# Turning v to rows in an attention block: one product of 64x128 of the array for four batches, in place of four of 64x32

## The chip, the cores and the metric

The kernel runs on one core of one Trainium2 chip. Its time is the device time of one execution in microseconds. The core has five engines with instruction streams of their own: TensorE (PE, matrix products; its weight loads are listed as PEld), VectorE (DVE), ScalarE (ACT), GpSimd (POOL) and SyncE (SP, which here only issues DMAs). They wait for each other by semaphores.

## The reference

One transformer block with adaptive layer norm, for 4 batches of 1024 steps of 256 channels:

- h = layernorm(x), scaled and shifted per batch
- q, k, v = silu(causal convolution with 4 taps of a projection of h to 1024 channels), that is 16 heads of 64; k is normalised; alpha and beta are sigmoids of projections of h
- a recurrence over the steps for each batch and head, on a 64x64 state S:

```
v_old = S k
S     = clip(alpha * S + beta * (v - alpha * v_old) k^T, -5, 5)
o     = S q
```

- o times a silu gate, a projection back to 256 channels, and a gated residual sum
- a second layer norm, a mixture of 8 experts of which each row uses 2, and a gated residual sum

## The kernel before

The kernel does the recurrence in 32 chunks of 32 steps. Two chunks, an even one (par 0) and an odd one (par 1), form a pair. Within a chunk the steps are solved at once through a triangular system, so that a chunk is a series of small matrix products and the state is carried from chunk to chunk. After the recurrence (function chunks, up to about 1890 us) follows the experts' part (function blocks), and after it two fallbacks that run only if the clip was in danger of acting.

The function chunks writes the order of the work itself: the scheduler is off for TensorE, VectorE, ScalarE and GpSimd (manual_schedule), and the letters of the string PLAN (line 56) say which of several generators takes its next step. In each of the 16 rounds, streams of two ages run side by side: passes (c), bounds (b) and below (l) finish the present pair, while rows, decays, keys_and_queries, values, triangle, rows_of_k and scaled (n, d, k, v, t, h, s) prepare the next one. SP's DMA issues are placed by the framework's scheduler.

The tiles that matter here hold four batches b of 32 steps, in one of two layouts. "Channels" has the channels of two heads on the partitions, a head p in each half of 64, and (batch, step) along the row: kq and v. "Rows" has (batch, step) on the 128 partitions, so that batch b is the quadrant of partitions 32b to 32b + 31 (quads), and the channels along the row: z, u, o. A product with a 64-row operand uses half of the rows of the array, and one with 32 columns of weights uses a quarter of its columns; the profile writes this as 64*32.

Steps that the change and the prediction touch, by line:

- L431, L441, L443, L449: projections and convolutions of k, q and v (ps_q on TensorE, then ScalarE and VectorE, then silu on ScalarE). L579 and L586: the gate's product, and its silu on ScalarE.
- L888 (in passes): v is turned to rows into ps_z, two PSUM tiles of 128x512, one per half p. The weights are v itself, the moving operand is a 64x64 identity. This opens an accumulation that L903 finishes with the product of k and the state; L912 copies it to z.
- L753, L756, L758 (end of triangle, VectorE): the solved triangular system and r_r are transposed.
- L810 and L822 (below): products of 32x32 and smaller for the off-diagonal blocks of the triangular solution; L810 needs Tn and the end of the VectorE steps above.
- L923, L937, L955, L974: u, the state's part of the output, the update of the state, the rest of the output. L1009: the output is transposed. L1025: the projection back.
- L352, L377, L378: the router's small products. L1063: u is transposed for the bounds. L1056: two loads per bounds step from a scratch tensor (aR, kR).

In an even chunk L888 is issued after L1009 of the chunk before and is followed by L810. In an odd chunk it is issued between a projection (L431) and a gate product (L579).

Of the kernel before, what the change touches and what calls it, by code (L numbers as in the profile page):

```python
# [212 lines left out]
def chunks(ctx, tc, a, nch, con, ones, modt, modc, x1_dram, n_safe, rt):  # L213

    nc = tc.nc
    GA, SB, CB = 0, 1, 2
    ident, iota8 = con["ident"], con["iota8"]
# [38 lines left out]
    half_p = lambda p: slice(p * 64, p * 64 + 64)  # L256
    quads = [slice(b * 32, b * 32 + 32) for b in range(B)]
# [614 lines left out]
    class Chunk:  # L872
# [3 lines left out]
        def passes(self, prev):  # L876

            pair, par, g = self.pair, self.par, self.pair.g
            kq, v, Tt, dq, kend = pair.kq, pair.v, pair.Tt, pair.dq, pair.kend[par]
# [4 lines left out]
            ps_z = [ps_c.tile([P, HP, DH], F32, name="ps_z", tag="c") for _ in range(2)]  # L884
            for hp in range(HP):
                for p in range(2):
                    for b, q in enumerate(quads):
                        nc.tensor.matmul(  # L888
                            ps_z[p][q, hp],
                            lhsT=v[hp // 2][half_p(p), hp % 2, par, b],  # L890
                            rhs=ident[half_p(p), half_p(p)],
                            start=(hp == 0),
                            stop=False,
                            skip_group_check=True,
                        )
            if par == 1:
                close("v", "v", "v", "v")
            yield
# [1 line left out]
            for hp in range(HP):  # L900
                for p in range(2):
                    for b, q in enumerate(quads):
                        nc.tensor.matmul(  # L903
                            ps_z[p][q, hp],
                            lhsT=kq[half_p(p), 0, hp, par, b],
                            rhs=S[half_p(p), b, hp],
                            start=False,
                            stop=True,
                            skip_group_check=True,
# [24 lines left out]
            for hp in range(HP):  # L934
                for p in range(2):
                    for b, q in enumerate(quads):
                        nc.tensor.matmul(  # L937
                            ps_o[p][q, hp],
                            lhsT=kq[half_p(p), 1, hp, par, b],
                            rhs=S[half_p(p), b, hp],  # L940
                            start=(hp == 0),
                            stop=False,
                            skip_group_check=True,
# [27 lines left out]
            for p in range(2):  # L971
                for hp in range(HP):
                    for q in quads:
                        nc.tensor.matmul(  # L974
                            ps_o[p][q, hp],
                            lhsT=dq[q, n_of(p, hp)],
                            rhs=u[q, hp, p],
                            start=False,
                            stop=True,
                            skip_group_check=True,  # L980
# [166 lines left out]
    def both_of(pair, prev):  # L1147
        chunks = [Chunk(pair, par) for par in range(2)]
        one = [prev] + chunks[:1]

        def passes():
            for c, before in zip(chunks, one):
                yield from c.passes(before)

        def bounds():
            for before in one:
                yield from before.bounds() if before else idle(14)

        return chunks[-1], passes(), bounds()
# [15 lines left out]
    for g in range(npair):  # L1175

        clear(3)
        prev, passes, bounds = both_of(now, prev)
        streams = dict(l=now.below(), c=passes, b=bounds, x=loads(2 * g + 6))
        if g + 1 < npair:  # L1180
            after, finished[:] = list(finished), []
            x = newer
            newer = [x_of.pop(2 * g + 4 + par) for par in range(2)] if g + 2 < npair else None
            now = Pair(g + 1, x, newer, after)
            streams.update(preparing(now))
        work(streams, PLAN)
# [721 lines left out]
```

## Time and profile before

| what | value |
|---|---|
| median of 3 runs | 2393.99 us (2391.24 to 2396.91) |
| profiled execution | 2413.01 us |
| its span, first to last instruction | 2411.1 us |
| mean granted TensorE clock | 0.826 |
| busy: PE, PEld | 1835.6 us (76%), 1491.0 us (62%) |
| busy: DVE, ACT, POOL | 1601.7 us (66%), 1008.6 us (42%), 1079.9 us (45%) |
| L888 on TensorE | 4096 records, 62.9 us busy, 21.6 us idle before them |

How to read it: the span is one execution seen by the hardware profiler; busy times of the engines overlap. A group line gives the source line, engine, operation, tiles, the part of the array (rows*columns), the shape of the moving operand, the count, then busy time in us and mean ns of one record, then the idle time of the engine before the group and what ended most of it. A record's ns includes its way through the array, and records overlap, so the rate is read from stretches, not from the mean. A line of waits gives in total us, times and longest us. A line of the timeline gives start and length in us, and in brackets the idle time before it and who ended it.

### The profile page before, as it was taken

Reading aid. Unit: us, or ns where it says so; the run is one execution under the profiler, and the core shown is the slowest. Engines: PE = TensorE matmul, PEld = TensorE weight load, DVE = VectorE, ACT = ScalarE, POOL = GpSimd, SP = SyncE. Lnnn points to the kernel's source line nnn. Section 1 sums busy time; section 2 is a strip of 40 time slices with the busy share of each in tenths; the row PEclk is TensorE's granted clock in tenths of the full one; section 3 lists DMA queues with packets and bytes.
Section 4 is the critical chain, followed back from the end, with each engine's and each line's share of the span. In section 5 each row is a group of like instructions: output and inputs, shape, how many; then the busy total and the mean of one; then the engine's idle time right before and its main releaser. Section 6 shows DMA issues by size and latency. Waiting matters only on the chain.

```text
span 2411.1 us, 96754 instructions
## 1 busy us (share of the span) xinstructions
PE 1835.6 (76%) x42550; PEld 1491.0 (62%) x42550; DVE 1601.7 (66%) x3170; ACT 1008.6 (42%) x2005; POOL 1079.9 (45%) x1189
## 2 busy tenths in 40 slices
PE   5677878787878787878687878878786716999930
PEld 3566656665767676766566666666675615888830
DVE  4768777878887868788777878897877323111124
ACT  3344545454544545455444444545443212222211
POOL 1115363637463636465545555564636450000046
PEclk7788878888978888889787979889887757999975
DMA  5513332425353434344434424242323105666636
GB/s 153 159 48 96 121 93 72 144 81 148 92 140 87 139 88 134 87 136 118 118 94 127 107 79 109 77 105 73 96 66 89 42 22 197 224 228 221 225 118 183
DMA packets 321248, 285.37 MB, mean 118 GB/s; under 512 B 112243, under 2 KB 279283, under 8 KB 320435
## 3 DMA queue, kind: packets, MB, share of 16 engines
q1 hardware_dynamic: 304946, 245.08, 35.5%
q0 software_dynamic: 9264, 27.01, 3.2%
q8 instruction: 337, 5.52, 0.9%
q10 hardware_dynamic: 6608, 7.00, 0.9%
q14 instruction: 93, 0.75, 0.1%
HBM read 215.09 MB, written 67.90 MB: 117 GB/s over the span
## 4 chain that ended last, share of the span: by engine, by line
PE 55%; issue 13%; DVE 8%; POOL 8%; DMA 7%; ACT 7%; SPq 2%; POOLq 0%; ACTq 0%; DVEq 0%
PE ps_q L431 16%; PE ps_hm L1670 6%; PE ps_yb L1682 5%; PE ps_w L1025 4%; PE ps_kk L647 3%; DMA sc<-g_scratch 3%; PE ps_gt L579 3%; PE ps_t L810 2%; PE ps_u L923 2%; PE ps_s L955 2%; POOL kq L792 2%; POOL aS L993 2%; DVE kq L443 2%; DMA y<-outs_scratch,at_out 1%; PE ps_o L974 1%
## 5 line engine op out<-in xcount | busy, mean ns | idle before, releaser
L443 DVE SCALAR_TENSOR_TENSOR kq<-ps_q,w_conv,kq 128x256 f32<-128x256 f32 x768 | 362.1, 482 | 132.8 <-ACT kq L441 112.1
L431 PE MATMUL ps_q<-hT,w_kq 128*128 128x280 f32 x1024 | 366.0, 507 | 32.4 <-issue 10.2
L431 PEld LDWEIGHTS ps_q<-hT,w_kq 128*128 128x128 f32 x1024 | 232.7, 241 | 110.2 <-issue 22.6
L443 DVE SCALAR_TENSOR_TENSOR v<-ps_q,w_conv,v 128x256 f32<-128x256 f32 x384 | 185.1, 482 | 70.4 <-ACT v L441 59.9
L441 ACT ACTIVATE kq<-ps_q,w_conv 128x256 f32<-128x256 f32 x256 | 143.5, 563 | 207.1 <-PE ps_q L431 205.0
L792 POOL TENSOR_TENSOR kq<-kq,sc 128x512 f32<-128x512 f32 x128 | 179.6, 1423 | 85.8 <-DMA sc<-g_scratch 82.3
L1096 DVE TENSOR_TENSOR_SCAN sides<-aR,sides 128x512 f32<-128x512 f32 x128 | 187.8, 1469 | 35.6 <-POOL sides L1089 34.9
L431 PE MATMUL ps_q<-hT,w_v 128*128 128x280 f32 x512 | 170.7, 461 | 36.9 <-ACT least L1073 21.7
L1088 POOL TENSOR_TENSOR sides<-sides,least 128x512 f32<-128x512 f32 x128 | 192.0, 1500 | 10.0
L1686 DVE TENSOR_TENSOR yb<-ps_yb,b 128x256 f32<-128x256 f32 x78 | 33.1, 424 | 244.2 <-PE ps_yb L1682 244.2
L993 POOL TENSOR_TENSOR aS<-S,last 128x1024 f32<-128x1024 f32 x64 | 127.1, 1986 | 137.5 <-DVE S L962 137.5
L1085 POOL TENSOR_TENSOR sides<-sides,kR 128x512 f32<-128x512 f32 x128 | 162.3, 1268 | 16.5 <-ACT sides L1071 16.4
L1677 ACT ACTIVATE hm<-ps_hm,b 128x256 f32<-128x256 f32 x156 | 73.8, 474 | 220.6 <-PE ps_hm L1670 220.5
L579 PE MATMUL ps_gt<-hT,w_gt 128*128 128x256 f32 x512 | 154.3, 427 | 4.0 <-issue 3.6
L1687 POOL DMA_DIRECT2D outs_scratch<-yb x39 | 27.9, 716 | 286.2 <-DVE yb L1686 276.5
L1670 PE MATMUL ps_hm<-hT,w 128*128 128x256 f32 x624 | 144.6, 385 | 9.1 <-DVE hT L1665 7.5
L1682 PE MATMUL ps_yb<-w,hm 128*128 128x256 f32 x624 | 141.0, 379 | 0.0
L431 PEld LDWEIGHTS ps_q<-hT,w_v 128*128 128x128 f32 x512 | 99.6, 213 | 66.3 <-ACT least L1073 31.8
L394 POOL DMA_INDIRECT rows_scratch<-ln_h,at x64 | 64.9, 1014 | 159.6 <-DVE at L391 79.9
L1670 PEld LDWEIGHTS ps_hm<-hT,w 128*128 128x128 f32 x624 | 117.9, 192 | 29.6 <-DVE hT L1665 14.2
L441 ACT ACTIVATE v<-ps_q,w_conv 128x256 f32<-128x256 f32 x128 | 72.0, 563 | 153.3 <-PE ps_q L431 150.4
L810 PE MATMUL ps_t<-Tn,kd 32*32 32x16 f32 x4096 | 63.4, 209 | 94.0 <-issue 53.8
(211 smaller groups left out, 3990.4 us busy)
## 6 DMA issues: line engine op xcount, KB each, us to landing
w<-in_w SPq DMA_DIRECT2D x78, 512.0 KB
rows_scratch<-zero_row SPq DMA_DIRECT2D x34, 1024.0 KB
w_kq<-in_w_qkv SPq DMA_DIRECT2D x260, 128.0 KB
sc<-g_scratch SPq DMA_DIRECT2D x128, 256.0 KB
w_v<-in_w_qkv SPq DMA_DIRECT2D x129, 128.0 KB
w_gt<-in_w_g SPq DMA_DIRECT2D x258, 64.0 KB
aR<-g_scratch SPq DMA_DIRECT2D x128, 128.0 KB
kR<-g_scratch SPq DMA_DIRECT2D x128, 128.0 KB
```

The source lines that it names most:

```text
L431: nc.tensor.matmul(ps.rearrange("p y t -> p (y t)"), lhsT=w[:, dc], rhs=h_t[:, dc].rearrange("p x b t -> p (x b t)"), start=(dc == 0), sto ...
L441: nc.scalar.activation(o, tap(0), AF.Identity, scale=taps[:, 0:1], bias=taps[:, KC : KC + 1])
L443: nc.vector.scalar_tensor_tensor(o, tap(j), taps[:, j : j + 1], o, op0=ALU.mult, op1=ALU.add)
L579: nc.tensor.matmul(ps, lhsT=wg[:, dc], rhs=self.h_t[:, dc, :, :, KC - 1 :].rearrange("p x b t -> p (x b) t"), start=(dc == 0), stop=(dc == 1),
L792: nc.gpsimd.tensor_tensor(o, o, sc[:, h4 : h4 + 4], ALU.mult)
L810: nc.tensor.matmul(ps[q, n], lhsT=kd[q, n], rhs=Tn[q, n], start=True, stop=True)
L993: nc.gpsimd.tensor_tensor(aS.rearrange("q b h i -> q (b h) i"), S[:, bs].rearrange("q b h i -> q (b h) i"), self.pair.last[self.par][:, bs ...
L1085: nc.gpsimd.tensor_tensor(grow, grow, kR.rearrange("q h b t -> q h (b t)"), ALU.mult)
L1088: nc.gpsimd.tensor_tensor(grow, grow, least, (ALU.subtract, ALU.add)[y])
L1096: nc.vector.tensor_tensor_scan(f, aR.rearrange("q h b t -> q (h b t)"), f, 0.0, ALU.mult, ALU.add)
L1670: nc.tensor.matmul(ps, lhsT=w1[:, dc, fc * P : (fc + 1) * P], rhs=hT[:, dc], start=(dc == 0), stop=(dc == 1),)
L1682: nc.tensor.matmul(ps, lhsT=hm[:, fc, s * P : (s + 1) * P], rhs=w2[:, fc], start=(fc == 0), stop=(fc == 3),)
```

## The change

The inner loop over the four batches goes. The four 64x32 weight operands, v[..., par, b] for b = 0 to 3, lie next to each other in a row, so they are taken as one operand of 64x128, and the output as all 128 partitions of ps_z[p] in place of one quadrant. The moving operand, the start and stop flags and the place in PLAN are as before.

```diff
             for hp in range(HP):
                 for p in range(2):
-                    for b, q in enumerate(quads):
-                        nc.tensor.matmul(
-                            ps_z[p][q, hp],
-                            lhsT=v[hp // 2][half_p(p), hp % 2, par, b],
-                            rhs=ident[half_p(p), half_p(p)],
-                            start=(hp == 0),
-                            stop=False,
-                            skip_group_check=True,
-                        )
+                    nc.tensor.matmul(
+                        ps_z[p][:, hp],
+                        lhsT=v[hp // 2][half_p(p), hp % 2, par].rearrange("q b t -> q (b t)"),
+                        rhs=ident[half_p(p), half_p(p)],
+                        start=(hp == 0),
+                        stop=False,
+                        skip_group_check=True,
+                    )
```

## The prediction

> **What bounds the kernel now.** I read first the page's span, its slices and its DMA queues.
>
> ```profile
> span 2411.1 us, 96754 instructions
> ...
> PE   5677878787878787878687878878786716999930
> ...
> q8 instruction: 337, 5.52, 0.9%
> ...
> PE 55%; issue 13%; DVE 8%; POOL 8%; DMA 7%; ACT 7%; SPq 2%; POOLq 0%; ACTq 0%; DVEq 0%
> ```
>
> The change sits in the first 1890 us, where the state is scanned in 16 rounds of about 110 us (two chunks each). TensorE is 70 to 80% busy there and holds most of the chain. The other thing to see is q8: 337 packets of 5.52 MB, so 16.4 KB each. TensorE's records are 2 x 42550 plus its waits, and 5.52 MB over these is 64 bytes each: q8 is TensorE's own instructions, arriving 256 at a time.
>
> Then the groups of the matmul engine, shapes kept apart.
>
> ```profile
> L888 PE MATMUL ps_z<-consts,v 64*32 64x64 f32 x4096 | 62.9, 269 | 21.6 <-issue 20.1 <-ACT v L449 1.1
> ```
>
> The 2048 products of L888 are 4096 records (each fp32 product runs in two passes), 128 records per chunk; with weight loads 256 instructions. "issue" is idle time that no wait explains.
>
> Then the waits, for what stands around L888:
>
> ```profile
> PE ps_t L810 <- issue: 53.8, 27, 3.1
> ...
> PE ps_t L810 <- DVE r_r L758: 35.6, 13, 5.7
> ```
>
> Last the timeline of TensorE, an even chunk (first four lines), an odd one (sixth), and rows for the costs:
>
> ```profile
> 1039.39 1.04 PE L888 MATMUL ps_z<-consts,v 64*32 64x64 f32 x62
> 1042.59 1.27 PE L888 MATMUL ps_z<-consts,v 64*32 64x64 f32 x66 [2.15 <-issue]
> 1045.73 1.04 PE L810 MATMUL ps_t<-Tn,kd 32*32 32x16 f32 x61 [1.87 <-DVE r_r L758]
> 1048.98 1.90 PE L810 MATMUL ps_t<-Tn,kd 32*32 32x16 f32 x128 [2.21 <-issue]
> ...
> 1086.91 0.61 PE L352 MATMUL ps_l<-w_router,hT 128*128 128x8 f32 x4
> 1087.45 1.16 PE L955 MATMUL ps_s<-u,kend 32*64 32x64 f32 x64
> ...
> 1091.14 0.60 PE L1063 MATMUL ps_ut<-consts,u 128*128 128x128 f32 x4
> ...
> 1102.44 1.13 PE L579 MATMUL ps_gt<-hT,w_gt 128*128 128x256 f32 x4
> ...
> 1107.98 1.75 PE L888 MATMUL ps_z<-consts,v 64*32 64x64 f32 x128
> ```
>
> In even chunks L888 is followed by L810, which waits for VectorE's transpose r_r (L758). In odd chunks it stands between a projection and the gate product L579, with nothing to wait for. The gaps of 2.15 and 2.21 us lie 66 + 61 = 127 pairs, or about 256 instructions, apart: the spacing of the q8 packets. TensorE runs out of instructions where they are short.
>
> **The change, part by part.** It replaces 64 products of 64x32 per chunk by 16 of 64x128 with the same 64 moving columns, so 128 records become 32 and 256 instructions 64. The order of TensorE, VectorE, ScalarE and GpSimd is otherwise unchanged. In SP's queue two aR loads (L1056) of one chunk pass one w_v and two w_gt issues; at 0.6 us per issue that is under 2 us, once, in a stream (bounds) that is used a chunk later: nothing, or 2 us if that cover fails.
>
> *Cost of a new record.* No 64x128 product is in the trace. Loading 128 columns of weights: L352 moves 8 columns and takes (0.61 - 0.29 for one record) / 3 = 0.11 us per record; L1063 moves 128 and takes (0.60 - 0.30) / 3 = 0.10. So at 8 moving columns it is the 128-column load that costs 0.11 us. At the half clock L1009 takes (1.97 - 0.42) / 7 = 0.22 us per record around 802 us, where the granted clock is 0.50. The new record loads 128 columns and moves 64, so it is bound by its load. The old one loaded 32, four tiles side by side; that is what the change gives away. Do the two 64-row halves load side by side? L955 has tiles in two row groups and two column halves: (1.16 - 0.23) / 63 = 15 ns per record, or 59 ns for four, hardly more than one 64-column load (half of 0.11). All four therefore load at once, row groups too. Ends: 55 ns per record with the halves side by side, 110 ns one after the other (110 and 220 at the half clock). I take 55, because L955 is the nearest row, and keep 110.
>
> [...] But L579, all in the same rows, takes (1.13 - 0.43) / 3 = 0.23 us for 256 columns, twice the 0.10 of L1063's 128, with no load added: the load is hidden. [...]
>
> *Odd chunks.* Before, sixteen stretches of L888 add up to 30.0 us in the timeline (1.57 to 2.66, mean 1.88, 0.14 of it gaps). After: 16 pairs x 0.11 + 0.3 for the last record = 2.06 us at full clock, 3.8 us for the last chunk, which runs at half: 15 x 2.06 + 3.8 = 34.7, or +4.7 us. The gate product and with it ScalarE (gate, v) come later by this; L377 behind it mostly waits 0.5 to 0.85 us for VectorE anyway. With TensorE's 55% of the chain for the share that shows: **+3 us**; ends 0 and +5.
>
> *Even chunks.* After: 16 x 0.22 + 0.4 = 3.9 us at the half clock. From the start of L888 to the end of r_r there are 4.3 to 8.7 us in the sixteen rounds (median 5.4), and L810 starts 0.1 us after r_r in nearly all. So nothing is lost, and 18 of the 20 us of gaps inside L888 that vanish were hidden by the same wait: **0**. If that cover went, it would cost 3.9 - 2.2 = 1.7 us per round.
>
> *Instruction blocks.* 4096 - 1024 = 3072 records and as many loads go: 6144 instructions, 24 of 337 packets. [...] Only what falls behind r_r counts, which is L810: 512 instructions, so two block ends in each round, most with a gap of 1.5 to 2.7 us. With 192 fewer instructions just before it, the block that L810 meets first has had longer to arrive. In the rounds at 1512 and 1617 us only one gap is left, and from L810's start to the end of L511 takes 6.6 and 6.8 us; the others take about 9.1. If each round lost one gap this would be 16 x 2.4 = 38 us; if gaps only move, 0. I take a quarter, four rounds: **-10 us**, near to the share of rounds (2 of 16) that show it, plus the odd chunks' 2 us.
>
> Sum: 3 + 0 - 10 = -7 us on the profiled span of 2411.1, so 2404 there (that execution was 2413.0). The median of the runs shown is 19 us lower, and I carry the difference over: 2394 - 7 = **2387 us**.
>
> **The rivals.** *The halves load in turn* (slower). 110/220 ns per record: an odd chunk takes 32 x 0.11 + 0.3 = 3.8 us, 1.9 more than before, x 16 x 0.55 = +17; an even one 7.1 to 7.4 us at the half clock against r_r after 4.3 to 8.7, in sum about +25 over the rounds. With the blocks' -10 that is +32: 2426 us. It is one mechanism, at L888, and decides from about 70 ns per record on (0.55 x 16 x (32 x 0.07 + 0.3 - 1.88) = 6 us in odd chunks, 2 to 4 in even ones, against 10). For it: no row shows 64x128. Against: L955.
> [...]
> *The gaps only move*: +3, 2397, no measurable change. For it: L810 keeps its 512 instructions and both of its block ends.
> *The gaps go in ten of sixteen rounds*: +3 - 24, 2373. For it: all rounds have one just behind L888.
> *The change does nothing*: excluded, for the instructions themselves differ.
>
> **How the numbers follow.** Forecast (2381 to 2393) 0.43; gaps only move 0.22; in turn 0.15; not hidden 0.12; many gaps go 0.08. About 0.2%, 5 us, is what can be told from no change. Faster: 0.36 of the forecast, the last 0.08 and 0.02 of others, 0.46. Same: 0.07 of the forecast, 0.14 of the moved gaps, 0.04 of the unhidden loads, 0.25. Slower: the rest, 0.29. The range of 2370 to 2412 leaves out the halves in turn (0.15) and the tail of the many gaps; the forecast's own range is 2379 to 2395.
>
> **What would show it.** L888 with 1024 records, an odd chunk taking 2.0 to 2.2 us, q8 with 313 packets; no more wait of L810 on L888 than before, the r_r wait longer; the issue gaps of L810 below 53.8 us. [...] The forecast is wrong if L810's gaps stay above 50 us, or if the clock falls: L888 in odd chunks runs at the full clock now.

## The result, and the profile after

The changed kernel takes 2370.79 us and the kernel before 2393.99 us (medians of 11 runs each): 23 us less, where 7 were forecast. The ratio used below is 0.9887 with a 95% interval of 0.9858 to 0.9916, 27 us; here and in every later ratio only fast runs count, which leaves out two of the 11 of the changed kernel, at 2383.9 and 2387.8 us, over 1.5% above its fastest. The profiled executions lie further apart than the medians (spans 2411.1 and 2353.9 us), since runs of one kernel differ by 0.7 to 1.7% among themselves; so single profiles are used below for what happens at one line, and timed runs for time.

The page of the changed kernel, in the lines that answer to those of before:

```profile
span 2353.9 us, 90609 instructions
...
q8 instruction: 313, 5.13, 0.9%
...
PE 52%; DVE 12%; issue 11%; ACT 8%; POOL 7%; DMA 7%; SPq 2%; ACTq 0%; POOLq 0%; DVEq 0%
```

24 instruction packets are gone, as counted, and "issue" on the chain falls from 13% to 11%.

That "issue" is mostly the wait for these packets can be read from their times in the traces. Up to 1890 us the kernel before has 133 issue gaps of TensorE over 0.4 us; 92% of them end 1.2 to 1.8 us after the end of a q8 packet (of the 107 in the changed kernel, 91%). Where two gaps lie one block of 256 instructions apart, exactly one packet stands between their ends, and in neither profile are these ends less than 3.45 us apart. So a block whose instructions are used up sooner is followed by a gap that fills this time:

```profile
1048.98 1.90 PE L810 MATMUL ps_t<-Tn,kd 32*32 32x16 f32 x128 [2.21 <-issue]
1052.45 1.14 PE L810 MATMUL ps_t<-Tn,kd 32*32 32x16 f32 x67 [1.57 <-issue]
```

From 1048.98 to 1052.45 are 3.47 us, for 1.90 us of products. Now the groups of the matmul engine (L887 is the changed line; L954 was L955):

```profile
L887 PE MATMUL ps_z<-consts,v 64*128 64x64 f32 x1024 | 92.6, 351 | 0.2 <-issue 0.2
L954 PE MATMUL ps_s<-u,kend 32*64 32x64 f32 x4096 | 88.4, 231 | 33.5 <-issue 32.7 <-DVE prod L739 0.7
...
L810 PE MATMUL ps_t<-Tn,kd 32*32 32x16 f32 x4096 | 62.1, 210 | 62.2 <-DVE r_r L758 32.2 <-issue 30.0
```

The changed products keep TensorE busy for 92.6 us where the old ones took 62.9, and still the kernel is faster. The issue gaps ahead of L810 fell from 53.8 to 30.0 us, those of L954 (the state's update) from 47.7 to 32.7, and those of the changed line itself from 20.1 to 0.2. Counted in the timelines, L810 has 18 such gaps in its 16 rounds where it had 27; rounds with two of them went from 11 to 2. The timeline of TensorE, an even chunk (first three lines) and an odd one:

```profile
1018.13 3.68 PE L887 MATMUL ps_z<-consts,v 64*128 64x64 f32 x32
1023.86 2.32 PE L810 MATMUL ps_t<-Tn,kd 32*32 32x16 f32 x157 [2.05 <-DVE r_r L758]
1027.86 1.57 PE L810 MATMUL ps_t<-Tn,kd 32*32 32x16 f32 x99 [1.69 <-issue]
...
1088.93 2.00 PE L887 MATMUL ps_z<-consts,v 64*128 64x64 f32 x32
```

The costs are as worked out: 2.00 us in the odd chunk (2.06 forecast), where the granted clock is 1.00, and 3.68 in the even one (3.9), where it is 0.50; this one ends 2.05 us before r_r lets L810 go. L810 has one gap here, where the round of before shown in the prediction has two (2.21 us, and 1.57 us at 1052 us). So the pieces were right and the total three times too small; the experiments ask where the rest comes from.

### The profile page after: what moved, and what is told of

Its sections match the earlier page's. It is cut to its first block, busy times and chain, and to the rows that moved or that the text cites. A ratio compares the mean times of both kernels' runs of the same rounds, so it can differ in the third digit from the quotient of the medians.

```text
span 2353.9 us, 90609 instructions
## 1 busy us (share of the span) xinstructions
PE 1833.1 (78%) x39478; PEld 1495.9 (64%) x39478; DVE 1595.8 (68%) x3170; ACT 1013.7 (43%) x2005; POOL 1086.7 (46%) x1189
## 4 chain that ended last, share of the span: by engine, by line
PE 52%; DVE 12%; issue 11%; ACT 8%; POOL 7%; DMA 7%; SPq 2%; ACTq 0%; POOLq 0%; DVEq 0%
PE ps_q L431 14%; PE ps_hm L1669 6%; PE ps_yb L1681 6%; DMA sc<-g_scratch 3%; PE ps_w L1024 3%; PE ps_kk L647 3%; PE ps_gt L579 3%; DVE kq L443 3%; PE ps_t L810 3%; PE ps_s L954 2%; POOL aS L992 2%; POOL kq L792 2%; PE ps_u L922 2%; PE ps_o L973 2%; PE ps_o L936 1%
## 5 line engine op out<-in xcount | busy, mean ns | idle before, releaser
L431 PE MATMUL ps_q<-hT,w_kq 128*128 128x280 f32 x1024 | 352.8, 491 | 34.8 <-issue 11.4
L431 PEld LDWEIGHTS ps_q<-hT,w_kq 128*128 128x128 f32 x1024 | 223.7, 232 | 110.4 <-issue 23.4
L431 PE MATMUL ps_q<-hT,w_v 128*128 128x280 f32 x512 | 161.0, 439 | 41.8 <-ACT least L1072 27.4
L579 PE MATMUL ps_gt<-hT,w_gt 128*128 128x256 f32 x512 | 147.9, 413 | 6.6 <-DMA w_gt<-in_w_g 2.5
L431 PEld LDWEIGHTS ps_q<-hT,w_v 128*128 128x128 f32 x512 | 93.7, 201 | 71.3 <-ACT least L1072 31.6
L1681 PEld LDWEIGHTS ps_yb<-w,hm 128*128 128x128 f32 x624 | 118.6, 190 | 16.1
```

Of the source, the lines that this page charges most:

```text
L431: nc.tensor.matmul(ps.rearrange("p y t -> p (y t)"), lhsT=w[:, dc], rhs=h_t[:, dc].rearrange("p x b t -> p (x b t)"), start=(dc == 0), sto ...
L579: nc.tensor.matmul(ps, lhsT=wg[:, dc], rhs=self.h_t[:, dc, :, :, KC - 1 :].rearrange("p x b t -> p (x b) t"), start=(dc == 0), stop=(dc == 1),
L1681: nc.tensor.matmul(ps, lhsT=hm[:, fc, s * P : (s + 1) * P], rhs=w2[:, fc], start=(fc == 0), stop=(fc == 3),)
```

## The experiments

Every ratio is to the kernel before, from runs on the same chip. Three theories came first to mind: A, only instructions ahead of L810 count; B, the fuller array holds a higher clock; C, every instruction taken out counts alike. D, E and F followed from later results.

**The change in even chunks alone, and in odd chunks alone.**

```diff
+                    if par == 0:    # the other kernel: par == 1
+                        nc.tensor.matmul(ps_z[p][:, hp], ...)    # 64x128
+                    else:
+                        for b, q in enumerate(quads):
+                            nc.tensor.matmul(ps_z[p][q, hp], ...)    # 64x32
```

> 64x128 products in even chunks only (the ones ahead of L810), 64x32 in odd ones. Theory A (the gain is the instructions that no longer stand ahead of L810): keeps nearly all of it, 0.985 to 0.991 of before, and the issue gaps of L810 are about 30 us as in the changed kernel. Theory B (the gain is the higher granted clock that comes with the fuller use of the array): half of it, 0.992 to 0.996. Theory C (every instruction taken out of the stream counts the same, wherever it stands): half of it, 0.993 to 0.995.

> The other half: 64x128 in odd chunks only. Theory A: no gain, 0.999 to 1.003 (the odd stretch is 0.2 us longer and on the path), issue gaps of L810 stay near 54 us. Theories B and C: 0.993 to 0.996.

Measured: even alone 0.9899 (0.9870 to 0.9928), odd alone 0.9884 (0.9840 to 0.9929). Each half has the whole gain, so the two don't add up. A falls as a theory of the time (odd alone should have had nothing), and B and C, which both wanted about half from each, don't explain the sum either. With even alone B has the clocks against it too: the mean granted clock of the runs was 0.834, and 0.835 in the kernel before beside it, at 1.0% less time (with odd alone it was 0.843). The groups of L810, even alone:

```profile
L810 PE MATMUL ps_t<-Tn,kd 32*32 32x16 f32 x4096 | 61.9, 210 | 75.9 <-DVE r_r L758 40.9 <-issue 35.0
```

and odd alone:

```profile
L810 PE MATMUL ps_t<-Tn,kd 32*32 32x16 f32 x4096 | 63.4, 209 | 90.3 <-issue 47.3 <-DVE r_r L758 43.0
```

At the line itself A is right: the gaps of L810 are near those of the changed kernel (30.0) where its own chunk is changed, and high where it is not. The time follows something else.

**The changed kernel with the instructions put back.** Tiny products whose results are overwritten before use, once ahead of L887, once ahead of the projection back:

```diff
+            if par == 0:    # ahead of L887; for the second kernel ahead of L1024, into ps_w, yT for v, rows half_p(0) alone
+                for i in range(48):
+                    q = quads[i % 4]
+                    nc.tensor.matmul(
+                        ps_z[i // 4 % 2][q.start : q.start + TH, HP - 1, :TH],
+                        lhsT=v[0][half_p(i // 4 % 2), 0, par, i % 4, :TH],
+                        rhs=ident[half_p(i // 4 % 2), :TH],
+                        start=True, stop=True, skip_group_check=True,
+                    )
```

> The changed kernel, with 48 tiny added products (64x16, 16 columns moved, overwritten before they are used) ahead of L887 in even chunks: the 192 instructions come back there, at some 0.8 us of array time that lies mostly behind the wait for r_r. Theory A: the gain is gone, 0.997 to 1.003, issue gaps of L810 back above 45 us. Theory B: the gain stays, 0.986 to 0.992. Theory C: half of it goes, about 0.994.

> The changed kernel, with the same 48 tiny added products ahead of L1024 (the projection back) of each even chunk instead, between long products. Theory A: instructions cost little there; their own array time of about 0.8 to 1.3 us per round is on the path, 16 x 0.55 x 1.0 = 9 us at most, so 0.989 to 0.994. Theory B: 0.989 to 0.993. Theory C: as in the kernel padded ahead of L887.

Measured: 0.9915 (0.9886 to 0.9944) and 1.0136 (1.0086 to 1.0186). Groups of the first:

```profile
L810 PE MATMUL ps_t<-Tn,kd 32*32 32x16 f32 x4096 | 64.0, 210 | 60.7 <-issue 46.9 <-DVE r_r L758 13.7
```

The gaps of L810 are back at 46.9 us, as A wanted, but little or nothing of the gain is lost. Theory A fails on the time for the second time. The other kernel was to be nearly free under every theory but C, and is 2.5% slower than the changed one. Its timeline shows a part of why:

```profile
1122.56 1.99 PE L922 MATMUL ps_u<-z,Tt 32*32 32x64 f32 x128
1124.48 1.13 PE L579 MATMUL ps_gt<-hT,w_gt 128*128 128x256 f32 x4
1125.54 0.31 PE L1026 MATMUL ps_w<-consts,yT 64*16 64x16 f32 x19
1127.46 0.79 PE L1026 MATMUL ps_w<-consts,yT 64*16 64x16 f32 x77 [1.61 <-issue]
```

The place is not among long products: 256 instructions of L922 (1.99 us) stand just ahead, and after 19 records of the added products TensorE stands 1.61 us on issue. Over the kernel these gaps are 24.5 us and the products themselves 17.7. The other issue gaps of TensorE grew as well, those of L954 from 32.7 to 51.1 us, so that in the group lines that name them they sum to 203.5 us, against 156.1 in the changed kernel. Gaps and products together have the size of the 60 us; how much of each lay on the path is not shown.

**The same instructions, with the block ends elsewhere.** Any edit of the count moves the end of every later block of 256 instructions, so each kernel so far differs from the kernel before in that too. To have this alone, tiny products go once ahead of the first round (32 of them are 128 instructions, half a block, 0.7 us of TensorE):

```diff
     to_channels(0, hs)
     halo(0)
+    ps = bank([P, TH], "ps_pad")
+    for i in range(32):    # 16, 48, 64 in the others
+        nc.tensor.matmul(
+            ps[quads[i % 4].start : quads[i % 4].start + TH],
+            lhsT=ident[half_p(0), :TH], rhs=ident[half_p(0), :TH],
+            start=True, stop=True, skip_group_check=True,
+        )
```

> The kernel before against itself, for what the comparison can tell on this kernel. All theories: 1.000 within 0.003.

> The kernel before with 32 tiny added products (128 instructions, half a block, about 1 us) once, ahead of the first round: every later block of 256 instructions ends half a block elsewhere. Theory D (the kernel before had its block ends in bad places, and any change of the count moves them: both halves of the change alone and the whole gain 1.1%, which does not add up): 0.988 to 0.995. Theory E (the instruction stream ran short, and either half takes away enough that something else bounds): 1.000 to 1.002.

> The changed kernel with the same 128 instructions ahead of the first round. Theory D: anywhere from 0.985 to 1.000, and not the same as the changed kernel. Theory E: the changed kernel's 0.989, within 0.003.

> The changed kernel again, on the chip of these comparisons. All theories: 0.989, within 0.003.

Measured: the kernel before against itself 1.0008 (0.9982 to 1.0033); shifted by half a block, with nothing else changed, **0.9902** (0.9866 to 0.9939); the changed kernel shifted 0.9925 (0.9887 to 0.9964), and again unshifted 0.9893 (0.9849 to 0.9936). Adding 128 instructions to the kernel before gains about as much as the change. E (the stream ran short, and either half relieves it) had wanted 1.000 and falls. Whether it is the place of the block ends, or something that the added products bring along, is told apart by a shift of a whole block:

> The kernel before with 64 tiny added products (256 instructions, a whole block) ahead of the first round: block ends fall where they did, one block later. Theory D (where block ends fall decides): 0.999 to 1.002, back at the kernel before. Theory F (it is not the place of the block ends but something else that the added products bring, such as another turn of the PSUM banks): 0.990, as with 32.

> The same with 16 products (64 instructions, a quarter of a block). Theory D: between 0.987 and 1.003, another place and so another time. Theory F: 0.990.

> The same with 48 products (192 instructions, three quarters of a block). Theory D: between 0.987 and 1.003; with the shifts of 0, a quarter and a half it gives the spread that the place alone makes in the kernel before, and the mean over places, against which the change is to be held: its own gain is what its mean over places has less. Theory F: 0.990.

> The changed kernel with 48 products ahead of the first round, a third place for it beside 0 (0.989) and half a block (0.9925). If the change has a gain of its own of about 0.3% as the working had it, the changed kernel's mean over places lies at 0.997 of the mean of the kernel before over its places; here 0.988 to 0.997.

> The changed kernel with 16 products (64 instructions, a quarter of a block) ahead of the first round, its missing fourth place. So far it stands at 0.989, 0.9925 and 0.9908 of the kernel before, whose own places stand at 1.000, 0.9977, 0.9902 and 0.9963. Place decides and the change has a gain of its own of 0.3 to 0.6%: 0.987 to 0.995. If the change had no gain of its own and its three places were lucky ones: 0.996 or more.

> The kernel before shifted by half a block, again. If the place decides: 0.990, within 0.004. If the first result was chance: 0.997 or more.

| shift, instructions | kernel before | changed kernel |
|---|---|---|
| 0 | 1.0008 (against itself) | 0.9887 and 0.9893 |
| 64 | 0.9977 (0.9951 to 1.0003) | 0.9945 (0.9915 to 0.9974) |
| 128 | 0.9902 and 0.9915 (0.9885 to 0.9944) | 0.9925 (0.9887 to 0.9964) |
| 192 | 0.9963 (0.9933 to 0.9993) | 0.9908 (0.9879 to 0.9936) |
| 256 | 0.9994 (0.9959 to 1.0028) | not run |

A whole block brings the kernel before back to itself, with twice the added products of the shift that gains 0.9% and the same one PSUM bank taken. So it is the place (D), not the products (F), and the gain at half a block came a second time on its repetition. In the groups, the kernel before shifted by 256:

```profile
L955 PE MATMUL ps_s<-u,kend 32*64 32x64 f32 x4096 | 87.1, 228 | 44.9 <-issue 44.1 <-DVE prod L739 0.7
L810 PE MATMUL ps_t<-Tn,kd 32*32 32x16 f32 x4096 | 63.6, 209 | 97.6 <-issue 56.5 <-DVE r_r L758 41.2
```

and by 128 (the repetition):

```profile
L955 PE MATMUL ps_s<-u,kend 32*64 32x64 f32 x4096 | 89.5, 233 | 41.4 <-issue 41.4
L810 PE MATMUL ps_t<-Tn,kd 32*32 32x16 f32 x4096 | 63.0, 209 | 88.4 <-issue 45.9 <-DVE r_r L758 42.5
```

The gaps of L810 shrink from 56.5 to 45.9 us by nothing but the shift; the other profiles agree (53.8 and 50.6 unshifted, 44.3 in the first one shifted by 128). Over the group lines of TensorE that name them the issue gaps sum to 208 to 217 us unshifted or shifted by 256, to 202, 190 and 205 us at 64, 128 and 192: least where the time is least, and most where it is most. The changed kernel at its slowest place, shifted by 64:

```profile
L954 PE MATMUL ps_s<-u,kend 32*64 32x64 f32 x4096 | 92.4, 237 | 45.5 <-issue 45.5
...
L810 PE MATMUL ps_t<-Tn,kd 32*32 32x16 f32 x4096 | 62.0, 210 | 64.3 <-issue 34.2 <-DVE r_r L758 30.1
```

Here the gap of L954 is as long as in the kernel before (it was 32.7 at the changed kernel's own place), but that of L810 stays low. Over the places the gaps of L810 are 44 to 57 us in the kernel before and 29 to 37 in the changed one: they don't overlap. That is the change's own doing. Over these lines the mean over four places is 203 us before and 170 after: of the 33 us, 14 are L810's and 17 the changed line's, and L954 keeps its own within 3 us. In the changed kernel the sums (158, 176, 161 and 183 us at 0, 64, 128 and 192) don't follow the times place by place.

"Place" must not be read as a fixed spot in each round. One round after the lines at 1045.73 of the kernel before and at 1023.86 of the changed kernel stand these, the first of before and the second of after:

```profile
1154.60 0.61 PE L810 MATMUL ps_t<-Tn,kd 32*32 32x16 f32 x31 [2.40 <-DVE r_r L758]
...
1135.86 2.75 PE L810 MATMUL ps_t<-Tn,kd 32*32 32x16 f32 x191 [2.32 <-DVE r_r L758]
```

The block ends 61 records into L810 in one round and 31 in the next; in the changed kernel 157 and then 191. So the ends move by about a quarter of a block (128 records) per round, from the third round on in both profiles, and each kernel meets all places in turn. A shift decides which round meets which place, and where in that turn the first and last rounds stand; why this is worth up to 0.9% is not shown.

The share of each: the mean over four places is 0.9962 before (1.000, 0.9977, 0.9909, 0.9963) and 0.9917 after (0.9890, 0.9945, 0.9925, 0.9908), a ratio of 0.9955. With about 0.003 on each value, 0.0015 on each mean and 0.002 on the ratio, the change is worth 0.45%, 11 us (6 to 15), at these four places. That interval holds the noise of the runs alone. Taken as a sample of all places, whose values differ by 0.9% before and 0.55% after, four of each leave about 0.5% of doubt (an estimate from that spread): the fewer gaps of L810 are clear of it, the 11 us are not. By these values the kernel before stands at the worst of its places (0.4% above its mean, 9 us) and the changed kernel at the best (0.27% below, 6 us), which makes the 1.1%; against the nearest places (64 before, 192 after) neither rank is clear of the noise.

**A projection in the wait.** The changed kernel, with one key projection moved ahead of L810 into the wait for r_r, to see whether more is to be had there:

```diff
-PLAN = "ccllnbddkkkncknb...
+PLAN = "cckllnbddkkncknb...
```

> The changed kernel with one k of the plan moved from just behind the two steps of below to just ahead of them: one key projection of each round (four records of L431, 2.2 us at the half clock) then runs in the wait for r_r. The wait was 32 us in all in the changed kernel, so if L810 still starts with r_r the projection is gained: 16 x 1.2 to 2.0 us, 0.979 to 0.983 of the kernel before. If the projection comes to delay L810, or its evacuation on ScalarE and VectorE delays r_r: no gain, 0.987 to 0.993.

Measured: 1.0067 (1.0025 to 1.0108), 1.8% slower than the changed kernel; neither case of the expectation. In the round shown L810 now waits 3.80 us for yT, and over the kernel ScalarE (L816) 75.7 us for L810's results, from 24.4. Its timeline of TensorE:

```profile
1035.18 2.23 PE L431 MATMUL ps_q<-hT,w_kq 128*128 128x280 f32 x4
1041.21 1.00 PE L810 MATMUL ps_t<-Tn,kd 32*32 32x16 f32 x60 [3.80 <-DVE yT L1013]
```

and of VectorE:

```profile
1036.79 0.17 DVE L758 STREAM_TRANSPOSE r_r<-rk 128x32 f32<-128x32 f32 x1
1036.87 3.61 DVE L1095 TENSOR_TENSOR_SCAN sides<-aR,sides 128x512 f32<-128x512 f32 x2
1040.40 1.26 DVE L1013 TENSOR_TENSOR yT<-ps_y,gate 128x512 f32<-128x512 f32 x2
```

r_r is ready at 1036.96, but L810 starts at 1041.21, within the second yT. The projection took one of the three PSUM banks that these steps use in turn, so L810's bank is now the one that L1008 filled and yT has still to read, and yT stands behind two scans on VectorE. No kernel measured here is clear of the changed one on the fast side.

## Why the prediction was right or wrong

- *Cost of a new record*, 55 ns with the halves side by side: right. 32 records took 2.00 us in the odd chunk, where the granted clock was 1.00, and 3.68 in the even one, where it was 0.50; less the 0.3 us that the prediction estimated for the last record, the odd chunk's are 53 ns each. One after the other would by the prediction's estimate have been 3.8 and 7.3 us; the decision by L955 and L579 stands. Loads that don't hide, to which the prediction gave 0.12, no run shows: the 53 ns leave no room for one beside the 55 of the estimate.
- *Odd chunks*, +3 us: the size of the stretch is right (2.00 us); what of it shows in the time was not measured apart.
- *Even chunks*, 0: right as to cover. L887 ends 2.05 us before r_r in the round shown. That the wait for r_r would grow was wrong: it is 32.2 us, from 35.6. With its gaps the old stretch took 3.4 us in the mean of the sixteen even chunks, so that the new one's 3.68 leaves the wait about where it was.
- *Instruction blocks*, -10 us: this is the term that failed. Its mechanism is right, fewer instructions ahead of L810 and so fewer gaps there: they are back at 46.9 us when the instructions are put back. Its size, "I take a quarter, four rounds", is not: in the pair of the result L810 lost 9 gaps and 24 us. Over the places it lost 14 us, against the 9.6 us of four rounds. With the +3 us the forecast of 7 is then not far from the 11 us at the four places.
- The same term had put nothing for what the new count does to all other block ends, and gave no reason. The time moves by up to 0.9% with it, and the starts of the two kernels gave another 15 us, by luck. The text had put the gaps exactly 256 instructions apart; with that, a step "and where will the ends lie after 192 instructions less per chunk" was due.
- Its reading of the two rounds with one gap less, from which the quarter was taken, was thin. The line of waits that it shows has 27 gaps of L810 in 16 rounds, so five rounds had one gap, though only those two were shorter. Nor is it the place of the ends alone: in these two the first block end came 68 and 38 records into L810, in the rounds at 1046 and 1155 us 61 and 31, and those had both gaps. The wait for r_r before them was longer, 3.34 and 3.19 us against 1.87 and 2.40. That fits with a block that had longer to arrive, but was not tested by itself.
- Of the rivals, "the halves load in turn" falls by the 2.00 us. "The gaps only move" falls as a mean over places, though at one pair of places (both kernels shifted by half a block, 0.991 and 0.9925) it would have seemed true. "The gaps go in ten of sixteen rounds", 2373, is nearest to the time, and nine gaps and 24 us did go in the pair of the result; but over the places it is 14 us, so that it was nearest by luck.
- The clock is not the cause. On the chip where both ran unshifted again, the mean granted clock of the runs was 0.838 in both, with a ratio of 0.9893. The two profiles first compared have 0.826 and 0.844, but the kernel before profiled again has 0.844 too. Half a block of shift came with 0.003 to 0.004 more clock; in the repeated runs of the kernel before 0.001 goes with 0.9 to 1.5 us, by the chip, so by this estimate 3 to 5 of its 20 us could be the clock.

Left open: why the order in which rounds and block ends meet is worth so much (the gaps of L954 and L955 move with it, 32.7 to 47.7 us, but shifted by 192 they have 43.7 and 43.8 us in the two kernels), and how much the two halves of the change are worth each over all places.

## What to carry to other kernels

Where TensorE runs many tiny products, count its instructions as well as its array time. The four small products took less of the array (1.75 us for an odd chunk, against 2.00), yet one wide product won here: it needs a quarter of the instructions, and where the array's longer time counted most, in the even chunks, it lay behind another engine's wait (in the round shown 3.68 us that ended 2.05 us ahead of r_r's release). Any edit of the count moves the block ends of everything after it; hold such a change against both kernels at several shifts, or part of what is measured is luck (here more than half, by the means over four places). Instructions that look free because long products are near can cost a gap if 256 short ones stand just ahead, as in the kernel padded at the projection back (24.5 us of them).

## What was not expected of the hardware

128 instructions put once at the start, 0.7 us of work, made a 2392 us kernel 0.9% faster, and 256 did nothing (0.9994). The instructions of TensorE arrive in 337 packets of 16.4 KB in the kernel before and 313 in the changed one, 256 instructions each (6144 instructions fewer made 24 packets fewer). Where small products used a block up sooner than 3.45 us, the least seen between the ends of two gaps a block apart, the engine stood for the rest of it at least: of the 133 gaps half lay between 0.9 and 1.9 us, the longest was 4.3, and over the kernel before those of L810, L955, L822 and L888 alone came to 154 us.
